# Four layers of recurrence and experts on one core: setup of layer 2's experts moved, three copies and scalings moved between engines, new prices in the instruction planner

## Chip, core and metric

One core of a Trainium2 chip runs the whole program. Its engines are TensorE (PE; its weight loads PEld), VectorE (DVE), ScalarE (ACT), GpSimd (POOL) and SyncE (SP), which here issues the transfers. The metric is the time of one execution in microseconds (us); of several runs the median is taken. The time before is 1239.51 us, the median of 3 runs (1238.63 to 1249.76).

## What is computed

Four layers on `x` of 2 x 1024 x 128, all in 32 bits. In each, the normalised input goes through a mixing part and a gating part:

```python
for layer in range(4):
    xn = layernorm(x)
    x = x + attn[layer](xn) * silu(ffn[layer](xn))
```

- Layer 0: a gated residual, a quantisation over groups, and a selective recurrence `h = h * exp(dt * A) + dt * x * B`, `y = sum(h * C)` over 16 states of 256 channels; beside it 8 experts with three matrices each.
- Layer 1: attention with global queries and keys; 8 experts, two of them chosen for each token.
- Layer 2: a convolution of 4 taps, then a recurrence in chunks with 32 heads of 64 and 128 states; 8 experts of width 64 with gelu and a shared one.
- Layer 3: causal attention and a feed-forward of width 512.

```python
# layer 2, the recurrence in chunks
Y_diag = (einsum('bcln,bcsn->bcls', C, B) * exp(segsum(A))) @ (dt * h)   # inside a chunk
states = einsum('bclhn,bclhp->bchpn', B * decay, dt * h)                 # what a chunk leaves
states = scan(states, decay_of_chunk)                                    # over the chunks
Y_off  = einsum('bcln,bchpn->bclhp', C, states) * exp(A_cum)             # from chunks before
y = (Y_diag + Y_off + D * h) * silu(gate)
```

## The kernel before

**Tiling.** Tokens lie in 16 tiles of 128. Features by tokens are handled in pieces of 512 columns, one bank of PSUM. A product that must be accurate is split: both factors into a rounded and a rest part (`split`, lines 541 and 542), and three matmuls (`mm3`, lines 553 to 555).

**Layer 0** (`take_1` to `take_5`, `inputs`, `step`). Each batch is done in two halves of 512 tokens, and each half in 16 steps `n` of two state groups. `take_1` makes `u`, the normalised input of a half, in four tiles with a scale and a shift for each row (line 946), turns it on TensorE, and hands it on. It runs two halves ahead, at step 14. `step` makes `dA` on ScalarE (line 1183), scans twice on VectorE (line 1184), and in the first half of each batch copies the last columns of `hs` into `last` (line 1186), from which the second half goes on. Then GpSimd multiplies `hs` in place by C (line 1187), and TensorE adds up the states into `y_ps` (line 1194). Layer 0's experts run beside it, and layer 1 of the first batch begins near its end.

**Layer 1** of the second batch (`layer_1`) alternates exponentials of the attention (line 663) and silu of the experts (line 721) on ScalarE.

**Layer 2** first makes features, batch constants (`batch_start`) and routing for both batches, in pools called `l2f` and `l2fw`. Then come its experts. Their weights are `fW1`, split in two; `pair`, a pattern that spreads the routing over an expert's rows, made from the scratch `pairf`; and the biases `b2s`. They stand in the pool `l2m`, opened after the features' pools; `pairf` takes the room of the gelu tiles `hw` in the pool `l2mw`. Lines 1581 to 1591 are the experts: `pb` from `pair`, `ph` from `fW1`, then the outputs.

Then 2 x 16 blocks of 128 features go through `front` (projection, convolution, silu), `weights` (the matrix `M` inside a chunk), `states` and `tail`. `states` turns `h` into `htok`, scales it on GpSimd (`hdd`, line 1662), multiplies to `u_ps` (line 1673), scans over chunks on VectorE (`st`, line 1674), and copies the states, turned about, into `stc` (line 1676): the first half on GpSimd, the second on ScalarE. `st` is read with a step of four elements. `tail` needs `M`, `htok` and `stc` for `yd_ps` and `yo_ps` (lines 1696 and 1701), adds and gates on VectorE and GpSimd (lines 1704 to 1713), and projects four blocks at a time (line 1720).

**What sets the order.** The program text gives only the dependencies. `_issue_order` plans every engine's queue: `_price` gives each instruction a duration, `_forward` runs a list planner over all engines with the tiles' rooms, `_backward` ranks instructions by the work behind them, and after 12 rounds the order with the shortest planned span is fixed, engine by engine. `SOONER` brings named parts forward. A pool whose room overlaps an older one waits, in the plan, for all of that one (`_pools_behind`); on the chip a tile waits for the tiles that it overlaps. ScalarE's queue is chosen so as to avoid changes of its function table.

## Time and profile before

| What | Value |
|---|---|
| Median of 3 runs | 1239.51 us |
| Profiled execution | 1244.13 us, span 1242.4 us |
| Layer 0: start and half 1; rest with layer 1 of batch 0 | 0 to 90; 90 to 470 |
| Layer 1 of batch 1, layer 2's first features | 411 to 625 |
| Layer 2's experts | 617 to 690 |
| Layer 2's blocks | 690 to 1157 |
| Layer 3 | 1147 to 1242 |

Times in the last five rows are from the first to the last instruction of the lines in question, so neighbours overlap. The page gives busy time by engine, then the span in 40 slices, one digit a slice:

```
PE   3797779877266888999999779899998998899998
DVE  6876997987999787678762578787897898889575
ACT  4455776765767784498743678778888778877554
POOL 6321777876657445122230257777885778887411
PEclk 9898989997667799999996889999999999998999
```

A digit is the busy share in tenths. VectorE is fuller than TensorE in slices 9 to 12, and from slice 17 on it is the other way. `PEclk` is the clock that TensorE was granted, in tenths of full speed; it falls with TensorE's activity in slices 9 to 13, and in slice 21 (652 to 683) while TensorE is busy. A row of a group reads: line, engine, operation, output and inputs with shapes, count | busy us in all, mean ns | idle us of the engine before them, and which instruction ended that idle time.

### The profile page before, as it was taken

The numbers are of one execution on the slowest core, as the hardware profiler recorded it, in microseconds if no ns is written. First come the engines' busy times: TensorE is split into PE (matmuls) and PEld (weight loads), VectorE is DVE, ScalarE is ACT, GpSimd is POOL, SyncE is SP. The second block draws the span as 40 slices with busy tenths as digits, with TensorE's granted clock in tenths as the row PEclk, the third lists the DMA queues.
The fourth block names the chain that finished last, engine by engine and source line by source line (L and its number), as shares of the span: only waits on it lengthen the run. The fifth ranks groups of instructions, "written<-read, shape, count | busy, mean of one in ns | idle before, by whom it ended". The sixth has DMA issues, their size and how long they took to land.

```text
span 1242.4 us, 18110 instructions
## 1 busy us (share of the span) xinstructions
PE 1044.9 (84%) x6415; PEld 754.5 (61%) x6415; DVE 980.4 (79%) x1618; ACT 862.0 (69%) x1258; POOL 687.5 (55%) x614
## 2 busy tenths in 40 slices
PE   3797779877266888999999779899998899998998
PEld 3564335444033666788766556667675767777687
DVE  6876997987999787678762578787897898889575
ACT  4455776765767784498743678778888778877554
POOL 6321777876657445122230257777885778887411
PEclk9898989997667799999996889999999999998999
DMA  3015343335342113110120323444443443442000
GB/s 104 7 38 143 100 150 130 115 132 171 132 153 93 51 44 97 41 40 17 58 80 7 104 72 85 113 114 131 123 115 90 108 111 93 116 115 63 18 9 26
DMA packets 58846, 109.15 MB, mean 88 GB/s; under 512 B 6274, under 2 KB 31746, under 8 KB 58628
## 3 DMA queue, kind: packets, MB, share of 16 engines
q1 hardware_dynamic: 58756, 108.00, 29.3%
q8 instruction: 51, 0.84, 0.3%
q14 instruction: 39, 0.32, 0.1%
HBM read 91.59 MB, written 14.29 MB: 85 GB/s over the span
## 4 chain that ended last, share of the span: by engine, by line
PE 37%; DVE 21%; ACT 11%; issue 5%; DMA 3%; POOL 2%; SPq 0%; DVEq 0%; POOLq 0%; ACTq 0%
DVE hs L1184 3%; DVE h L1350 3%; PE y_ps L730 3%; PE wo_ps L1720 3%; PE u_ps L1673 3%; PE yd_ps L1696 2%; DVE st L1674 2%; PE yo_ps L1701 2%; PE in_ps L553 2%; PE in_ps L555 2%; PE in_ps L554 2%; PE y_ps L1589 1%; PE e_ps L1637 1%; ACT L721 1%; PE ht_ps L1658 1%
## 5 line engine op out<-in xcount | busy, mean ns | idle before, releaser
L1187 POOL TENSOR_TENSOR hs<-hs,bc 128x1024 f32<-128x1024 f32 x64 | 153.5, 2403 | 97.0 <-DVE hs L1184 41.6
L1350 DVE SCALAR_TENSOR_TENSOR h<-in_ps,w,h 128x1023 f32<-128x1023 f32 (+2 forms) x96 | 121.9, 1272 | 26.1 <-ACT h L1347 25.7
L1183 ACT ACTIVATE dA<-dd,negA 128x512 f32<-128x512 f32 x128 | 87.5, 689 | 50.6 <-DVE hs L1184 43.9
L730 PE MATMUL y_ps<-w2e,hh 128*128 128x128 f32 x512 | 79.8, 293 | 14.5 <-DVE acc L735 6.0
L1674 DVE TENSOR_TENSOR_SCAN st<-cd,u_ps 128x512 f32<-128x512 f32 x64 | 77.7, 1213 | 17.3 <-PE u_ps L1673 9.7
L730 PEld LDWEIGHTS y_ps<-w2e,hh 128*128 128x128 f32 x512 | 72.0, 203 | 30.2 <-DVE hh L722 11.3
L1640 DVE SCALAR_TENSOR_TENSOR M<-e_ps,GT 128x1024 f32<-128x1024 f32 x64 | 76.9, 1214 | 15.7 <-ACT e_ps L1638 13.8
L1662 POOL TENSOR_TENSOR hdd<-htok,dtd 128x512 f32<-128x512 f32 x64 | 68.2, 1067 | 37.5 <-ACT htok L1661 34.5
L1184 DVE TENSOR_TENSOR_SCAN hs<-dA,last,dBx 128x512 f32<-128x512 f32 x64 | 79.5, 1268 | 7.4 <-PE y_ps L1194 4.0
L1707 POOL TENSOR_TENSOR h<-h,so 128x384 f32<-128x384 f32 (+1 forms) x64 | 73.0, 1143 | 18.8 <-DVE so L1706 18.6
L1708 POOL TENSOR_TENSOR h<-h,sg 128x512 f32<-128x512 f32 x64 | 81.7, 1282 | 0.8
L1701 PE MATMUL yo_ps<-Cf,stc 128*128 128x128 f32 x448 | 75.3, 284 | 8.1 <-DVE so L1706 2.9
L1184 DVE TENSOR_TENSOR_SCAN hs<-dA,dBx 128x512 f32<-128x512 f32 x64 | 75.4, 1207 | 5.7 <-PE y_ps L1194 4.3
L1713 POOL TENSOR_TENSOR ssq<-ssq,so 128x512 f32<-128x512 f32 x60 | 76.3, 1280 | 5.0 <-ACT so L1712 4.7
L1701 PEld LDWEIGHTS yo_ps<-Cf,stc 128*128 128x128 f32 x448 | 64.6, 193 | 19.3 <-DVE so L1706 3.9
L1696 PE MATMUL yd_ps<-M,htok 128*64 128x128 f32 x1024 | 71.8, 284 | 4.9 <-DVE wo L1722 2.5
L1673 PE MATMUL u_ps<-hdd,Btok 128*128 128x128 f32 x448 | 70.6, 281 | 6.0 <-issue 3.1
L1673 PEld LDWEIGHTS u_ps<-hdd,Btok 128*128 128x128 f32 x448 | 63.1, 193 | 18.1 <-issue 9.8
L553 PE MATMUL in_ps<-xh,w_in_l 128*128 128x512 f32 x128 | 60.8, 477 | 13.2 <-ACT sg L1620 5.1
L1175 DVE TENSOR_TENSOR dBx<-dd,B_ps 128x1024 f32<-128x1024 f32 x48 | 58.0, 1208 | 12.0 <-DMA dd<-dt 6.6
L1696 PEld LDWEIGHTS yd_ps<-M,htok 128*64 128x64 f32 x1024 | 56.1, 139 | 18.1 <-DVE wo L1722 3.6
L1638 ACT ACTIVATE e_ps<-e_ps 128x1024 f32<-128x1024 f32 x64 | 63.8, 1012 | 1.6 <-PE e_ps L1637 1.0
(533 smaller groups left out, 3220.9 us busy)
## 6 DMA issues: line engine op xcount, KB each, us to landing
bc<-BCd SPq DMA_DIRECT2D x32, 512.0 KB
cd<-Dd SPq DMA_DIRECT2D x32, 512.0 KB
so<-So SPq DMA_DIRECT2D x64, 256.0 KB
dd<-Dtd SPq DMA_DIRECT2D x28, 512.0 KB
w13f<-in_w13d_dram SPq DMA_DIRECT2D x16, 256.0 KB
Dtd<-dt SPq DMA_DIRECT2D x7, 512.0 KB
fw<-in_fwd_dram SPq DMA_DIRECT2D x16, 192.0 KB
dd<-dt SPq DMA_DIRECT2D x4, 512.0 KB
```

What stands on the lines that cost most here:

```text
L553: nc.tensor.matmul(out, wl, xh, start=start, stop=False)
L730: nc.tensor.matmul(y_ps[:, j * P : (j + 1) * P], hh[:, c, j * P : (j + 1) * P], w2e[:, c * P : (c + 1) * P], start=(c == 0), stop=(c == 1))
L1183: nc.scalar.activation(dA, dd[:, r, 0, :], AF.Exp, scale=negA[:, n, r : r + 1])
L1184: nc.vector.tensor_tensor_scan(hs[:, r, :], dA, dBx[:, r, :], last[:, n, r : r + 1] if h else 0.0, ALU.mult, ALU.add)
L1187: nc.gpsimd.tensor_tensor(hs, hs, cs.to_broadcast([P, 2, 512]), ALU.mult)
L1350: nc.vector.scalar_tensor_tensor(dst[:, n:], ps[:, : S - n], w[:, k : k + 1], dst[:, n:], ALU.mult, ALU.add)
L1640: nc.vector.scalar_tensor_tensor(M, ps, 3.0e38, G, ALU.min, ALU.mult)
L1673: nc.tensor.matmul(pv[:, j, :], Btok[:, c, :], hdd[:, c, :], start=True, stop=True)
L1674: nc.vector.tensor_tensor_scan(st.rearrange("p f j -> p (f j)"), cd[:, half].rearrange("p h w -> p (h w)"), ps, 0.0, ALU.mult, ALU.add)
L1696: nc.tensor.matmul(yd[64 * k : 64 * (k + 1), j * P : (j + 1) * P], htok[:, 4 * q + j, 64 * k : 64 * (k + 1)], Ms[q][:, k, j * P : (j + 1) ...
L1701: nc.tensor.matmul(yo[:, j * P : (j + 1) * P], stc[:, c - 1, :], Cf[:, c * P : (c + 1) * P], start=True, stop=True)
L1708: nc.gpsimd.tensor_tensor(y, y, sg[:, cols], ALU.mult)
```

## The change

Four things, and the order of all queues with them, as the planner runs anew.

1. The experts' weights of layer 2 move from after the features to before them, into a pool `l2m` that opens before `l2f`. The raw `fW1` borrows the room of `xnT`, the scratch `pairf` that of `v2`, both in `l2f`. The gelu tiles' pool `l2mw` stays where it was in the text, and shifts in memory by 2560 bytes.
2. The states' second half and `last` are copied by GpSimd, not by ScalarE.
3. `u` is scaled on ScalarE, not on VectorE and GpSimd in turn.
4. `_price` gets other durations: a fixed cost higher by 107 ns for ScalarE and by 81 ns for VectorE, prices of their own for scans, for narrow and stepped matmuls, and a lower one for GpSimd's copies.

```diff
 def _price(op, reads, writes, in_psum):
...
-        return 2 + 0.4167 * (max(n, 2 * rows) if "float32r" in str(ins.ins[0].dtype) else 4 * max(n, rows))
+        odd = 215.0 if reads[0].ap[0][1] % 32 else 250.0 if any(abs(list(a.ap)[-1][0]) > 1 for a in reads) else 0.0
+        return odd + 2 + 0.4167 * (max(n, 2 * rows) if "float32r" in str(ins.ins[0].dtype) else 4 * max(n, rows))
...
     if op.engine == "Activation":
-        return (52 if in_psum(reads[0]) else 93) + 0.8333 * n + 93 * (scalars + len(writes) - 1)
+        return (159 if in_psum(reads[0]) else 200) + 0.8333 * n + 93 * (scalars + len(writes) - 1)
     if op.engine == "DVE":
...
-        fast = ins.opcode in ("TensorScalarPtr", "TensorCopy") and full <= 1 and not any(map(in_psum, reads + writes))
-        return 69 + (0.5208 if fast else 1.0417) * n + 61 * min(scalars, 2)
+        near = any(map(in_psum, reads + writes))
+        if getattr(ins, "is_tensor_tensor_scan", False):
+            return 130 + (2.1 if near else 2.4) * n
+        fast = ins.opcode in ("TensorScalarPtr", "TensorCopy") and full <= 1 and not near
+        share = 1.0 if near else 1.2
+        return 150 + (0.5208 if fast else 1.0417) * share * n + 61 * min(scalars, 2)
     if ins.opcode == "TensorTensor":
-        return 120 + 2.16 * n
+        return 120 + 2.3 * n
...
-    return 112 + (3.3 if ins.opcode == "TensorCopy" else 1.0) * n
+    return 112 + (2.0 if ins.opcode == "TensorCopy" else 1.0) * n
...
                 for j, t in enumerate(ts):
-                    eng = nc.gpsimd if j % 2 else nc.vector
-                    eng.tensor_scalar(u[:, j, :], qx[:, t, :], rinv[:, j : j + 1], shift[:, j : j + 1], ALU.mult, ALU.add)
+                    nc.scalar.activation(u[:, j, :], qx[:, t, :], AF.Identity, bias=shift[:, j : j + 1], scale=rinv[:, j : j + 1])
...
                 if h == 0:
-                    nc.scalar.copy(last[:, n, :], hs[:, :, 511])
+                    nc.gpsimd.tensor_copy(last[:, n, :], hs[:, :, 511])
...
-        with pool_of("w2early", side="right") as pe, pool_of("l2f", side="right") as pf, pool_of("l2fw", bufs=2, side="right") as pw, lead:
+        with pool_of("w2early", side="right") as pe, pool_of("l2m", side="right") as pex, pool_of("l2f", side="right") as pf, pool_of("l2fw", bufs=2, side="right") as pw, lead:
...
+            mark("moe_2_weights")
+            fW1 = split_pair(pex, apart(pf, "fW1", "xnT"), "fW1")
+            pairf = pf.tile([P, 2, 4, 2, 64], F32, name="pairf", tag="v2", bufs=2)[:16]
...
+            pair = pex.tile([16, 4, P], F32R, name="pair")
...
             features(0)
...
-            mark("moe_2_weights")
-            pf, pw = lead.enter_context(pool_of("l2m", side="right")), lead.enter_context(pool_of("l2mw", bufs=2, side="right"))
+            pw = lead.enter_context(pool_of("l2mw", bufs=2, side="right"))
...
-            fW1 = split_pair(pf, apart(pf, "fW1", "fW1"), "fW1")
-            pairf = pw.tile([P, 2, 4, 2, 64], F32, name="pairf", tag="hw")[:16]
...
-                    (nc.scalar.copy if half else nc.gpsimd.tensor_copy)(stc[:, 4 * half : 4 + 3 * half, :], st[:, :, half:].rearrange("p f j -> p j f"))
+                    nc.gpsimd.tensor_copy(stc[:, 4 * half : 4 + 3 * half, :], st[:, :, half:].rearrange("p f j -> p j f"))
```

More of the change, by code (lines that the diff above doesn't have):

```diff
@@ L1516, in routing @@
                     nc.scalar.copy(wT[:, b * S + q * 512 : b * S + (q + 1) * 512], ps[:26, :])
+            mark("moe_2_weights")
+            fW1 = split_pair(pex, apart(pf, "fW1", "xnT"), "fW1")
+            pairf = pf.tile([P, 2, 4, 2, 64], F32, name="pairf", tag="v2", bufs=2)[:16]
+            nc.gpsimd.memset(pairf, 1.0)
+            for h in range(2):
+                nc.gpsimd.affine_select(out=pairf[:, h], in_=pairf[:, h], pattern=[[-2, 4], [-1, 2], [0, 64]], compare_op=ALU.is_equal, fill=0.0, base=-8 * h, channel_multiplier=1)
+            pair = pex.tile([16, 4, P], F32R, name="pair")
+            nc.vector.tensor_tensor(pair, pairf[:, 0].rearrange("k p a b -> k p (a b)"), pairf[:, 1].rearrange("k p a b -> k p (a b)"), ALU.add)
+            b2h = pex.tile([26, P], F32R, name="b2h")
+            b2l = pex.tile([26, P], F32, name="b2l")
+            nc.scalar.copy(b2h, W2a["b2s"][:26, :])
+            nc.vector.tensor_tensor(b2l, W2a["b2s"][:26, :], b2h.bitcast(F32), ALU.subtract)
+            low = pex.tile([26, 3], F32, name="low")
+            nc.gpsimd.affine_select(out=low[:, 0:1], in_=ones[:26, 0:1], pattern=[[0, 1]], compare_op=ALU.is_ge, fill=0.0, base=-16, channel_multiplier=1)
+            nc.gpsimd.affine_select(out=low[:, 1:2], in_=ones[:26, 0:1], pattern=[[0, 1]], compare_op=ALU.is_equal, fill=0.0, base=-24, channel_multiplier=1)
+            nc.vector.tensor_tensor(low[:, 2:3], low[:, 0:1], low[:, 1:2], ALU.subtract)
+            nc.vector.tensor_tensor(b2l, b2l, b2h.bitcast(F32), ALU.subtract)
+            b2s = pex.tile([26, P], F32R, name="b2s")
+            nc.vector.scalar_tensor_tensor(b2s, b2l, low[:, 2:3], b2h.bitcast(F32), ALU.mult, ALU.add)
             features(0)
@@ L1540, in recurrent_d4 @@
                 nc.vector.tensor_copy(Mr[32:40].rearrange("r c l -> r (c l)"), patm)
-            mark("moe_2_weights")
-            pf, pw = lead.enter_context(pool_of("l2m", side="right")), lead.enter_context(pool_of("l2mw", bufs=2, side="right"))
+            pw = lead.enter_context(pool_of("l2mw", bufs=2, side="right"))
             pm = lead.enter_context(pool_of("l2m_ps", bufs=3, space=PSUM, side="right"))
             pmy = lead.enter_context(pool_of("l2m_y", bufs=1, space=PSUM, side="right"))
-            fW1 = split_pair(pf, apart(pf, "fW1", "fW1"), "fW1")
-            pairf = pw.tile([P, 2, 4, 2, 64], F32, name="pairf", tag="hw")[:16]
-            nc.gpsimd.memset(pairf, 1.0)
-            for h in range(2):
-                nc.gpsimd.affine_select(out=pairf[:, h], in_=pairf[:, h], pattern=[[-2, 4], [-1, 2], [0, 64]], compare_op=ALU.is_equal, fill=0.0, base=-8 * h, channel_multiplier=1)
-            pair = pf.tile([16, 4, P], F32R, name="pair")
-            nc.vector.tensor_tensor(pair, pairf[:, 0].rearrange("k p a b -> k p (a b)"), pairf[:, 1].rearrange("k p a b -> k p (a b)"), ALU.add)
-            b2h = pf.tile([26, P], F32R, name="b2h")
-            b2l = pf.tile([26, P], F32, name="b2l")
-            nc.scalar.copy(b2h, W2a["b2s"][:26, :])
-            nc.vector.tensor_tensor(b2l, W2a["b2s"][:26, :], b2h.bitcast(F32), ALU.subtract)
-            low = pf.tile([26, 3], F32, name="low")
-            nc.gpsimd.affine_select(out=low[:, 0:1], in_=ones[:26, 0:1], pattern=[[0, 1]], compare_op=ALU.is_ge, fill=0.0, base=-16, channel_multiplier=1)
-            nc.gpsimd.affine_select(out=low[:, 1:2], in_=ones[:26, 0:1], pattern=[[0, 1]], compare_op=ALU.is_equal, fill=0.0, base=-24, channel_multiplier=1)
-            nc.vector.tensor_tensor(low[:, 2:3], low[:, 0:1], low[:, 1:2], ALU.subtract)
-            nc.vector.tensor_tensor(b2l, b2l, b2h.bitcast(F32), ALU.subtract)
-            b2s = pf.tile([26, P], F32R, name="b2s")
-            nc.vector.scalar_tensor_tensor(b2s, b2l, low[:, 2:3], b2h.bitcast(F32), ALU.mult, ALU.add)
             for q in range(NQ):
```

## The prediction

> **What bounds the kernel now.** I read the page first, then busy time by stage, then the groups of instructions by shape, the waits, and last the order of time around two places. The profiled execution took 1244.13 us (span 1242.4 and 1.7 around it), 0.37% over the median of 1239.51; sums below are made against 1244.13 and scaled at the end.

> The page's first part says that no engine is near its span:

> ```profile
> PE 1044.9 (84%) x6415; PEld 754.5 (61%) x6415; DVE 980.4 (79%) x1618; ACT 862.0 (69%) x1258; POOL 687.5 (55%) x614
> ```

> Busy time by stage (columns: stretch; length; busy us of PE, PEld, DVE, ACT, POOL; granted clock; DMA share; GB/s) shows two limits. Layer 0's recurrence (90 to 411) is VectorE's, 282.6 of 321 us; from 498 to 1150 it is TensorE's, 143.7 of 152 and 412.2 of 460 us.

> ```profile
> 90.00:411.00 321.00, 233.06 (x1167) 123.34 (x1165) 282.61 (x330) 225.49 (x378) 213.14 (x122) 0.84 0.41 131
> 498.00:650.00 152.00, 143.71 (x903) 117.00 (x902) 113.20 (x299) 108.22 (x175) 36.46 (x38) 1.00 0.15 47
> 690.00:1150.00 460.00, 412.19 (x2929) 316.17 (x2928) 381.13 (x432) 365.62 (x446) 335.56 (x326) 0.97 0.39 104
> ```

> The groups that the change moves (count, then busy us and mean ns, then idle before them):

> ```profile
> L946 DVE TENSOR_SCALAR u<-qx,ln_y,shift 128x128 f32<-128x128 f32 x8 | 8.2, 1050 | 0.0
> L852 ACT ACTIVATE qx<-X,shift,ln_y 128x128 f32<-128x128 f32 x12 | 4.7, 479 | 3.6 <-DVE shift L819 3.6
> L1186 ACT COPY last<-hs 128x2 f32<-128x2 f32 x32 | 5.9, 186 | 13.6 <-DVE hs L1184 13.6
> L1676 POOL COPY stc<-st 128x512 f32<-128x512 f32 x32 | 35.9, 1120 | 27.2 <-DVE st L1674 27.2
> L1676 ACT COPY stc<-st 128x384 f32<-128x384 f32 x32 | 28.8, 901 | 10.7 <-DVE st L1674 10.7
> ```

> The tile view of u gives the spread of those eight VectorE rows (minimum, median, maximum ns): the mean of 1050 comes from a few long ones.

> ```profile
> L946 DVE TENSOR_SCALAR u<-qx,ln_y,shift x8: 311/342/2471, 61.9 to 229.4; 128x128 f32<-128x128 f32 x8
> ```

> The waits (us in total, times, longest): over the span, of VectorE in 90 to 411, and of TensorE in 690 to 1150.

> ```profile
> POOL hs L1187 <- ACT last L1186: 31.1, 12, 8.2
> ```

> ```profile
> DVE hs L1184 <- PE y_ps L1194: 8.4, 7, 2.9
> ```

> ```profile
> PE in_ps L553 <- ACT sg L1620: 5.1, 3, 4.1
> PE ht_ps L1658 <- ACT htok L1661: 3.3, 4, 1.7
> PE yo_ps L1701 <- ACT stc L1676: 2.4, 4, 1.1
> PE e_ps L1637 <- ACT sg L1620: 1.8, 3, 1.1
> ```

> **Part by part.** A, scaling u on ScalarE. VectorE loses 8 instructions, GpSimd 8 (6.8 us), ScalarE gains 16 of the L852 row, 16 x 0.479 = 7.7 us. VectorE sets the recurrence, and 6 of its 8 lie there, between 90.5 and 229.4. These took 7.7 us of the group's 8.2 (the two before are 0.34 each); that is the worth if the long ones vanish, and 6 x 0.342 = 2.1 if their stalls fall on the next instruction instead. I take 5, between the two: the sum is measured, but the stall's owner is not shown. On ScalarE, 70% busy there, the 16 queue among the exponentials dA; only the next half's transposes wait for u, which leaves no loss to count, and the first take has four in a row, 1.9 us, and the two engines took 2.1 (61.8 to 63.9). **-5** (0 to -7.7).

> B, last columns on GpSimd. ScalarE loses 32 x 0.186 = 5.9 us. GpSimd gains 32 small copies; none of this shape exists there, and the nearest rows, 128x3 copies of the halo (L956) at 0.184 and 0.416, give 5.9 to 13.3 us; I take 0.2 each, 6.4 us. The 31.1 us that GpSimd waited for ScalarE end, because copy and product now follow each other in one queue. But GpSimd is 66% busy there, so only what reaches VectorE counts: at most the 8.4 us in which its scans waited for y_ps. I take a quarter. Queued behind the copy are the product hs and then y_ps; if that 0.2 came through in full for the half that is not hidden, it would cost 3. **-2** (-8.4 to +3).

> C, second half of the states on GpSimd. ScalarE loses 28.8 us. GpSimd's row is 1120 ns for 512 elements, 2.19 ns each, so 384 take 0.84 us and 32 of them 26.9 us. Its busy share in 690 to 1150 goes from 335.6 to 362.5 of 460, 73 to 79%; ScalarE's falls from 79 to 73%. The copy itself is as fast as before (0.84 against 0.90). On TensorE's path lie the four waits for ScalarE above, 12.6 us; a lighter queue saves at best all of them, and I take 3, a quarter, since each is ended by one late instruction and not by the load as such. Against it: behind the copy in GpSimd's queue stand hdd and the two products of h, and the copy waits behind them; a 1.28 us product ahead of every copy, with a quarter reaching TensorE, is 32 x 1.28 / 4 = 10. **-3** (-12.6 to +10).

> [...]

> D, experts' weights set up earlier. Now the scratch of pair sits in the room of the gelu tiles, which overlaps layer 1's buffers, so it is made at 617.5 to 620.5, after layer 1's last matmuls, and the first pb runs at 621.05. In the changed program pair comes before layer 1's end. TensorE had other work then and idled only 0.54 us: that is the gain; bounds 0 and 3 (the whole delay). The gelu tiles still overlap layer 1 by 6 KB, so the experts cannot start much sooner. The second place is the gap behind the first experts, in order of time:

> ```profile
> 649.86 0.32 PE L1591 MATMUL y_ps<-b2s,wT 26*128 26x128 f32 x1
> 653.11 1.19 PE L1386 MATMUL cum_ps<-Adt,gt 128*128 128x256 f32 x2 [2.93 <-DVE sel L594]
> ```

> Another 0.72 go by before er_ps (655.03), which waits for the routing's w26. As stretches again (the clock is the third column from the right),

> ```profile
> 655.00:670.00 15.00, 14.97 (x37) 9.20 (x38) 3.17 (x5) 5.35 (x9) 0.00 (x0) 0.50 0.00 0
> 670.00:675.00 5.00, 5.00 (x23) 3.82 (x23) 0.02 (x1) 0.92 (x2) 0.00 (x0) 0.75 0.00 0
> ```

> After 3.65 us of idling the clock is at a half for 17.5 us and more with TensorE full, so some 9 to 10 us are lost. The new order puts about 2.6 us of small matmuls (k_ps 0.43 and 0.42, ct_ps 0.64, half of er_ps) behind layer 1's last outputs, which would fill the first gap; but it also sets two VectorE steps that wait for ScalarE (nlog, dtd, with a table load of 1.28 between) ahead of the routing, which opens the second by some 2 us. I keep the loss. **-0.5** (-10 to +3). Early loading costs nothing: the raw weights borrow xnT's room, split by 488.5 and needed by xnT at 544.9, and W_BC, now behind them in SP's queue, is split at 520.

> [...]

> E, prices and the new order. The planner's prices come nearer to the rows (a ScalarE pass of 512 from SBUF 627 ns for 520; row L1712: 632), but price no time by themselves. What can be counted is the new queue: table loads fall from 166 to 160, by 7 up to the last dA and by 3 from there to layer 1's end, against 2 more in layer 2 and 2 in layer 3. Those before layer 1's end lie on the chain of waits, where Exp and Silu alternate:

> ```profile
> 538.76 1.28 ACT L721
> 540.05 0.60 ACT hh L721
> 540.67 1.28 ACT L663
> ```

> 3 x 1.28 = 3.8 us there; the seven in the recurrence hide beside VectorE, the four late ones beside TensorE. Bounds: all six net, -8, and as much again the other way for an order that has more waits. **-4** (-8 to +8).

> Sum: -5 - 2 - 3 - 0.5 - 4 = -14.5: 1229.6 for the profiled execution, times 1239.51/1244.13, **1225** for the median.

> **Rivals.** Hidden (0.18): the removed ScalarE work was off the path. For it: TensorE is at 94% from 498 to 650 and 90% after 690, ScalarE in no stretch of 100 us above 82%. Against it: the chain above. Only A's lower end remains, 2.1 us: 1237 (1233 to 1242).

> GpSimd becomes late in layer 2 (0.22, slower): yo_ps waits for both halves of the states, now in one queue with hdd, two products of h and ssq. Price: all 26.9 us added come onto the path, less the 11.5 of A, B, D and E, +15.4: 1255 (1246 to 1262). For it: in 1000 to 1100 GpSimd was already 81% busy. It decides once yo_ps waits more than 15 us for GpSimd's stc.

> The half clock goes (0.12): the gap at 650 stays under 2 us, 10 us more are won: 1215 (1207 to 1222). For it the 2.6 us of filling; against it the delayed routing.

> That a part does not do what it says holds for D: the weights were never in layer 1's room, only their scratch, so D is priced at next to nothing.

> **Numbers.** The sum as it stands has 0.48 (1216 to 1236). One per cent, 12.4 us, is about what can be told from no change. Below 1227 lie 0.34 of the first case and all of the last: faster 0.46; within, 0.14 and the hidden case: same 0.32; slower 0.22. The range 1209 to 1254 leaves out some 0.08 below and 0.12 above.

> **What would show it.** A: VectorE's busy time in the recurrence down by 5 or more and the last scan, now at 470, some 7 us sooner. B: no wait of hs for last. C: stc rows on GpSimd near 0.84 us, yo_ps waiting under 5 us for them. D: pair before layer 1's end, the clock still at a half after the first experts. E: 160 table loads. I am wrong if VectorE's sum falls and the scan does not end sooner, or if TensorE's idle time in layer 2 (48 us now) grows by more than 10.

## The result, and the profile after

The changed kernel takes 1250.16 us, the median of 20 runs (1242.02 to 1257.64); the kernel before, run beside it, 1242.32 (20 runs). The ratio is 1.0063, 95% interval 1.0044 to 1.0082: slower by some 0.6%, where 1225 and a gain were forecast. The profiled execution took 1251.49 us, its span is 1249.8, against 1242.4 before: 7.4 us more.

The page's busy time of the whole span. VectorE has 7 us more than before, in 8 instructions fewer; ScalarE has 31 us less, GpSimd 29 us more, as the moved copies would have it.

```profile
PE 1061.0 (85%) x6415; PEld 766.6 (61%) x6415; DVE 987.1 (79%) x1610; ACT 830.6 (66%) x1204; POOL 716.9 (57%) x670
```

Busy time by stage, with the columns of before (stretch; length; PE, PEld, DVE, ACT, POOL; granted clock; DMA share; GB/s). The figure that stands out is the clock of the second line, 0.90 where it was 1.00. TensorE's idle time in the third fell from 47.8 us to 41.5.

```profile
90.00:411.00 321.00, 241.34 (x1158) 124.89 (x1158) 290.51 (x330) 223.67 (x357) 217.45 (x148) 0.83 0.40 132
498.00:650.00 152.00, 140.05 (x802) 113.92 (x800) 104.10 (x281) 95.25 (x156) 31.29 (x31) 0.90 0.15 45
690.00:1150.00 460.00, 418.50 (x2983) 323.17 (x2982) 384.28 (x429) 343.73 (x418) 358.31 (x355) 0.98 0.39 105
```

The groups that were moved: u on ScalarE, last and the states' second half on GpSimd. The scaling costs what the row of before gave (0.484 us, for 0.479 assumed); the copies cost a little more than assumed (0.230 and 0.889 us, for 0.2 and 0.84).

```profile
L1682 POOL COPY stc<-st 128x512 f32<-128x512 f32 x32 | 35.9, 1121 | 8.5 <-DVE st L1680 8.5
L1682 POOL COPY stc<-st 128x384 f32<-128x384 f32 x32 | 28.4, 889 | 6.4 <-DVE st L1680 6.4
L1191 POOL COPY last<-hs 128x2 f32<-128x2 f32 x32 | 7.4, 230 | 39.4 <-DVE hs L1189 19.1 <-DMA dd<-Dtd 15.3 <-DVE ln_t L538 3.6
L951 ACT ACTIVATE u<-qx,shift,ln_y 128x128 f32<-128x128 f32 x16 | 7.3, 484 | 0.0
```

The tile view of u (minimum, median, maximum ns): the long ones are gone.

```profile
L951 ACT ACTIVATE u<-qx,shift,ln_y x16: 479/482/505, 69.4 to 243.1; 128x128 f32<-128x128 f32 x16
```

Waits in 90 to 411 (total, times, longest): GpSimd's copy now waits for the scans themselves, and the scans no longer wait for y_ps.

```profile
POOL last L1191 <- DVE hs L1189: 19.1, 10, 4.6
DVE hs L1189 <- ACT dA L1188: 5.0, 4, 2.5
```

TensorE's waits in 690 to 1150. For the states on GpSimd it waits 2.4 us, as long as it did for ScalarE.

```profile
PE in_ps L559 <- ACT sg L1626: 5.9, 2, 4.1
...
PE yo_ps L1707 <- POOL stc L1682: 2.4, 3, 1.2
...
PE ht_ps L1664 <- ACT htok L1667: 0.8, 2, 0.5
PE e_ps L1643 <- ACT sg L1626: 0.4, 1, 0.4
```

So where is the time? The table holds the end of an instruction, in us from the span's start, for both kernels and for two of the experiments below:

| End of | before | after | e1 | e3 |
|---|---|---|---|---|
| last scan of the recurrence | 471.2 | 460.9 | 463.5 | 461.9 |
| layer 1's last output matmul | 617.8 | 613.0 | 615.3 | 614.0 |
| layer 1's last X += acc | 625.6 | 624.7 | 627.0 | 625.7 |
| layer 2's last expert output | 689.6 | 707.0 | 694.7 | 690.7 |
| first convolution of the blocks | 693.7 | 711.2 | 699.0 | 695.0 |
| layer 3's first projection | 1156.9 | 1164.3 | 1153.1 | 1147.9 |
| last X | 1239.3 | 1246.6 | 1235.4 | 1230.2 |

The recurrence is 10.3 us sooner. 5.5 of that goes by layer 1's last output, 3.9 between it and the last addition. From there to the first convolution 86.5 us pass instead of 68.1: 18.4 lost. The blocks then take 453.1 instead of 463.2, 10.1 won; layer 3 is the same. The result is one loss of 18 us in the experts of layer 2, larger than either gain. Windows of the clock show it (columns as above):

```profile
626.00:650.00 24.00, 23.23 (x65) 15.65 (x64) 9.97 (x40) 4.61 (x8) 2.52 (x5) 0.51 0.26 71
650.00:684.00 34.00, 29.14 (x94) 21.81 (x94) 11.80 (x30) 12.83 (x19) 4.89 (x5) 0.50 0.04 16
```

The trace's clock records have TensorE at half clock from 626.4 to 684.5, 58.0 us, where before it was 652.1 to 672.5, 20.5 us. It is busy nearly throughout, but in a run of 512-column matmuls each starts 0.43 us after the one before, not 0.23. 37.5 us more at half clock are 18.8 us of work: the 18.4.

What stands at the start of that stretch? Of TensorE's waits in 612 to 632, two lie there. The first, for `hw` (the gelu of an expert's hidden values times `pb`), ends at 625.37, before the fall; the second ends at 628.45, behind it.

```profile
PE y_ps L1595 <- DVE hw L1589: 1.2, 1, 1.2
PE ph L559 <- ACT hsh L1584: 0.8, 1, 0.8
```

And VectorE's queue in order of time there. The last addition of layer 1 waits 1.90 us for acc and then takes 1.63, and the second product hw stands behind it. In the kernel before two products run first, at 622.12 and 623.19, then the addition at 624.41.

```profile
620.50 0.69 DVE L1589 TENSOR_TENSOR hw<-hw,pb 128x512 f32<-128x512 f32 x1
623.08 1.63 DVE L757 TENSOR_TENSOR X<-X,acc 128x1024 f32<-128x1024 f32 x1 [1.90 <-POOL acc L756]
624.64 0.67 DVE L1589 TENSOR_TENSOR hw<-hw,pb 128x512 f32<-128x512 f32 x1
```

The gap between the experts of the two batches, shown for before in the prediction, has shifted behind: 1.67 and 3.19 us of waiting, for 2.93 and 0.72.

```profile
671.51 1.19 PE L1391 MATMUL cum_ps<-Adt,gt 128*128 128x256 f32 x2 [1.67 <-DVE Adt L1389]
675.89 1.86 PE L1520 MATMUL er_ps<-ident,w 128*26 128x128 f32 x8 [3.19 <-DVE w L1516]
```

### The profile page after: what moved, and what is told of

Same layout as the page of the kernel before. It is cut to its first block, busy times and chain, and to the rows that moved or that the text cites. A ratio compares the mean times of both kernels' runs of the same rounds, so it can differ in the third digit from the quotient of the medians.

```text
span 1249.8 us, 18115 instructions
## 1 busy us (share of the span) xinstructions
PE 1061.0 (85%) x6415; PEld 766.6 (61%) x6415; DVE 987.1 (79%) x1610; ACT 830.6 (66%) x1204; POOL 716.9 (57%) x670
## 5 line engine op out<-in xcount | busy, mean ns | idle before, releaser
L1192 POOL TENSOR_TENSOR hs<-hs,bc 128x1024 f32<-128x1024 f32 x64 | 154.1, 2410 | 51.5 <-DVE hs L1189 27.3
L1355 DVE SCALAR_TENSOR_TENSOR h<-in_ps,w,h 128x1023 f32<-128x1023 f32 (+2 forms) x96 | 121.9, 1270 | 16.0 <-ACT h L1352 15.4
L1646 DVE SCALAR_TENSOR_TENSOR M<-e_ps,GT 128x1024 f32<-128x1024 f32 x64 | 76.6, 1215 | 15.2 <-ACT e_ps L1644 14.7
L736 PE MATMUL y_ps<-w2e,hh 128*128 128x128 f32 x512 | 76.9, 291 | 8.7 <-DVE hh L728 7.3
L1713 POOL TENSOR_TENSOR h<-h,so 128x384 f32<-128x384 f32 (+1 forms) x64 | 73.3, 1148 | 15.5 <-DVE so L1712 15.4
L1707 PE MATMUL yo_ps<-Cf,stc 128*128 128x128 f32 x448 | 70.5, 285 | 2.9 <-POOL stc L1682 2.4
L1682 POOL COPY stc<-st 128x512 f32<-128x512 f32 x64 | 64.3, 1005 | 14.9 <-DVE st L1680 14.8
L559 PE MATMUL in_ps<-xh,w_in_l 128*128 128x512 f32 x128 | 60.4, 473 | 10.7 <-ACT sg L1626 5.9
L1199 PE MATMUL y_ps<-hs,fold 128*32 128x512 f32 x256 | 54.7, 715 | 17.3 <-POOL hs L1192 17.1
```

What stands on the lines that cost most here:

```text
L736: nc.tensor.matmul(y_ps[:, j * P : (j + 1) * P], hh[:, c, j * P : (j + 1) * P], w2e[:, c * P : (c + 1) * P], start=(c == 0), stop=(c == 1))
L1192: nc.gpsimd.tensor_tensor(hs, hs, cs.to_broadcast([P, 2, 512]), ALU.mult)
L1355: nc.vector.scalar_tensor_tensor(dst[:, n:], ps[:, : S - n], w[:, k : k + 1], dst[:, n:], ALU.mult, ALU.add)
L1646: nc.vector.scalar_tensor_tensor(M, ps, 3.0e38, G, ALU.min, ALU.mult)
L1707: nc.tensor.matmul(yo[:, j * P : (j + 1) * P], stc[:, c - 1, :], Cf[:, c * P : (c + 1) * P], start=True, stop=True)
```

## The experiments

The theory after this: the loss is the longer half clock, begun by TensorE's wait at 624 to 625, which the planner made by putting the addition ahead of hw. The rivals: the chain itself is late, whatever the clock; or one of the four parts costs by itself. Ratios are to the kernel before, run beside each, with 95% intervals; the stretches are those of the profiled execution.

**e1, e2: one instruction moved.** After planning, one instruction is taken out of VectorE's queue and put in elsewhere; e1 from the changed kernel, e2 the mirror from the kernel before.

```diff
+    for what, where, side in moves:
+        order.remove(op)
+        order.insert(order.index(ref) + side, op)
# e1: (second hw, last X += acc, 0)   e2: (last X += acc, second hw, 0)
```

> The changed kernel with one instruction moved in VectorE's queue: layer 1's last X += acc stands behind the second product hw of layer 2's first expert quarter, as in the kernel before, not ahead of it. Theory (the loss is the longer stretch at half clock, 58.0 us against 20.5, begun by TensorE's wait of 1.16 us for that product): TensorE no longer waits for hw at 625, the clock holds past 626 to about 650, the half-clock stretch is 20 to 35 us, the last expert output ends near 690 instead of 707, and the time is 1232 to 1242, a ratio to the kernel before of 0.992 to 1.000. Rival (the chain of the later routing and the table loads at layer 1's end is late whatever the clock): the last expert output stays at 704 to 708, the time at 1247 to 1253, ratio 1.004 to 1.008.

> The mirror of it: the kernel before with layer 1's last X += acc moved ahead of the second product hw in VectorE's queue; nothing else. Theory: TensorE waits about 1 us for hw near 625, the clock is halved at once and stays half for 45 to 60 us instead of 20.5, the first convolution starts at 702 to 712 instead of 693.7, and the time is 1248 to 1260, ratio 1.005 to 1.014. Rival (this order costs its wait and no more): 1241 to 1244, ratio 0.999 to 1.002.

e1: 1237.05 us, 0.9918 (0.9885 to 0.9951). The stretch begins at 656 again and lasts 20.5 us:

```profile
626.00:650.00 24.00, 22.32 (x121) 16.51 (x121) 15.00 (x52) 9.85 (x17) 5.97 (x9) 1.00 0.35 95
650.00:684.00 34.00, 27.52 (x96) 17.73 (x94) 12.41 (x28) 11.35 (x17) 3.65 (x3) 0.70 0.02 8
```

One VectorE instruction in another place is worth 1.4% (1.0063 to 0.9918), and the change without this accident is a gain. The last output missed its mark (694.7, for "near 690").

e2: 1248.59 us, 1.0029 (1.0002 to 1.0056), between the two expectations. In its profiled execution TensorE waits 1.82 us for hw, the clock falls at 629.6 and is back after 3.4 us, and the experts end at 689.7 as before; but there the fall in the second gap lasts only 10.2 us, against 20.5 before. The mean granted clock of its 12 runs has a median of 0.9215, against 0.926 before, and the runs part into six of 1243.7 to 1246.9 us (0.922 to 0.927) and six of 1250.3 to 1255.1 (0.914 to 0.921); the profiled one is of the first six. So the order begins a fall; that it lasts longer in some executions than in others is inferred from the mean clock, as one alone was profiled.

**e3, e5: idling filled.** Spare matmuls into a tile that nobody reads, in TensorE's queue alone; the output is computed as before.

```diff
+                    for k in range(8):
+                        nc.tensor.matmul(warm, fW1[0][:, :P], xh[:, cols], start=True, stop=True)
# e3: five ahead of the waiting y_ps, three ahead of the waiting ph; e5: two, ahead of ph alone
```

> The changed kernel with eight spare matmuls into a tile that nobody reads: five in TensorE's queue ahead of the output that waits 1.16 us for hw, three ahead of the product that waits 0.77 us behind it. All other queues, the late addition in VectorE's among them, stay as they are. Theory (the clock falls because TensorE itself is idle there, whatever it is fed with): the clock holds past 626, the half-clock stretch is 20 to 35 us, the last expert output ends at 689 to 698, the time is 1233 to 1242, ratio to the kernel before 0.992 to 0.999. Rival (it is the order of the additions and the later chain, not the clock): as the changed kernel or worse, 1248 to 1254, ratio 1.004 to 1.009.

> The changed kernel with two spare matmuls only, in TensorE's second gap (0.77 us ahead of the product ph at 628); the first gap of 1.16 us, for hw, stays. It asks what makes the stretch long. Theory (the first gap starts it, the second keeps the clock down): the clock still falls near 626 but is back within 4 to 25 us, time 1238 to 1246, ratio 0.996 to 1.001. Rival (the length does not hang on the second gap): 45 to 60 us at half clock, time 1247 to 1254, ratio 1.004 to 1.009.

e3: 1237.52 us, 0.9944 (0.9921 to 0.9966). The eight (row of the group in 612 to 632) take 2.2 us, in place of the two waits:

```profile
L1618 PE MATMUL warm<-xh,fW_h 128*128 128x512 f32 x8 | 2.2, 396 | 0.0
```

```profile
626.00:650.00 24.00, 23.92 (x129) 17.68 (x127) 14.99 (x53) 9.78 (x18) 4.77 (x9) 1.00 0.32 89
650.00:684.00 34.00, 28.04 (x114) 18.56 (x114) 13.75 (x30) 11.93 (x17) 3.65 (x3) 0.80 0.02 8
```

The y_ps that waited starts at 626.38, 1.01 later than after, and layer 1's last output ends 1.0 later too; nothing was brought forward. Yet the last expert output ends 16.3 us sooner. The clock holds to 654.9 and is then at a half for 13.7 us, less than the 20 to 35 expected. The other engines' queues, the chain and every price are those of the changed kernel; beside the spare matmuls only the clock differs. This settles it against the rival chain.

e5: 1238.61 us, 0.997 (0.9938 to 1.0002), as the theory had it, though its 12 runs fall apart: nine between 1235.0 and 1239.4 with a mean clock of 0.925 to 0.931, three between 1246.4 and 1250.3 at 0.916 to 0.919. The profiled one is of the three (20.5 us at half clock from 629.6, and 13.7 more at 663.7). So two matmuls in the second wait are worth 0.9% (1.0063 to 0.997), though the first wait still begins a fall; how long it lasts in the executions that were not profiled is not shown.

**p1 to p5: the parts.** p1 is the kernel before with the new `_price`; p2 the changed kernel with the old one; p3 the changed kernel without the early weights; p4 the kernel before with u, last and the states' copies moved; p5 with the early weights only. Their diffs are those parts of the diff above.

> The kernel before with the new prices alone (u, last, the state copies and the experts' weights stay as before). The planner then also puts X += acc ahead of the second product hw. Theory: the early half clock comes from the prices alone; without what the moved copies save, the time is 1250 to 1262, ratio 1.006 to 1.016. Rival (the prices are harmless, and a moved copy or the weights cost it): 1236 to 1245, ratio 0.995 to 1.002.

> The changed kernel with the old prices: u on ScalarE, last and both state copies on GpSimd, the experts' weights set up early. The planner then keeps X += acc behind both products hw. Theory: the clock holds to about 650 and the recurrence's gain of some 10 us is kept for the most part: 1228 to 1239, ratio 0.989 to 0.998. Rival (a moved part costs by itself): 1245 to 1255, ratio 1.002 to 1.010.

> The changed kernel with the experts' weights of layer 2 left where they were before (new prices, u on ScalarE, last and states on GpSimd stay). The planner still puts X += acc ahead of the first products hw. Theory (the early half clock comes from the prices' order, not from where the weights are set up): the half clock begins near 627 to 635 again and the time is 1246 to 1258, ratio 1.002 to 1.012. Rival (the early weights brought it): 1232 to 1241, ratio 0.991 to 0.998.

> The kernel before with u on ScalarE and last and both state copies on GpSimd, and nothing else: old prices, weights where they were. In the changed kernel with old prices, layer 2's blocks took 487 us from the first convolution to layer 3's first scores, against 463 before and 453 after. Theory (GpSimd's copies at the old price of 3.3 ns an element are planned badly, whatever the weights do): the blocks take 475 to 495 us, the last scan of the recurrence ends near 460, and the time is 1252 to 1268, ratio 1.006 to 1.019. Rival (the early weights spoil the blocks): 1230 to 1240, ratio 0.989 to 0.997.

> The kernel before with the experts' weights of layer 2 set up early, and nothing else: old prices, all copies where they were; the planner keeps X += acc behind both products hw. Theory (the early weights are harmless, the late addition lengthens the half clock): the half-clock stretch of the experts is 10 to 25 us, the time 1240 to 1246, ratio 0.998 to 1.002. Rival (the early weights themselves lengthen it, as the changed kernel without them was faster than with them): stretch over 35 us, time 1248 to 1257, ratio 1.004 to 1.012.

| | u, last, stc | weights | prices | us | ratio (interval) | last scan | blocks | at half clock in the experts |
|---|---|---|---|---|---|---|---|---|
| before | | | | 1242.32 | 1 | 471.2 | 463.2 | 20.5 |
| p5 | | x | | 1243.00 | 0.9993 (0.9973 to 1.0012) | 470.7 | 465.8 | 10.2 |
| p1 | | | x | 1259.63 | 1.0110 (1.0078 to 1.0142) | 477.2 | 458.9 | 27.3 + 20.5 |
| p4 | x | | | 1275.99 | 1.0247 (1.0219 to 1.0276) | 461.6 | 491.7 | 10.2 |
| p2 | x | x | | 1263.79 | 1.0135 (1.0101 to 1.0169) | 458.0 | 487.1 | 10.2 |
| p3 | x | | x | 1241.02 | 0.9972 (0.9947 to 0.9997) | 458.4 | 453.2 | 10.2 + 20.5 |
| after | x | x | x | 1250.16 | 1.0063 (1.0044 to 1.0082) | 460.9 | 453.1 | 58.0 |

"Blocks" is the time from the first convolution to layer 3's first projection. p1 has the time that the theory named, and p4 lies 8 us above its range. p2 was expected at 1228 to 1239 and missed by 25 us: its experts end early (last output at 682.3), but its blocks are 34 us longer than after's. p3 was expected slow and is not: its ratio is the rival's, and its early fall lasts 10.2 us.

The theory's reason does not hold in p1 and p3, although both plans put the addition ahead of hw. In neither trace does TensorE wait for hw before the early fall (635.5 in p1, 621.3 in p3). It waits for the routing `wT`, which ScalarE copies; first p1, then p3:

```profile
633.14 0.49 PE L1587 MATMUL pb<-wT,pair 16*128 16x512 f32 x1 [1.83 <-ACT wT L1522]
```

```profile
619.95 0.50 PE L1586 MATMUL pb<-wT,pair 16*128 16x512 f32 x1 [1.46 <-ACT wT L1521]
```

In p1 the addition starts only at 635.10. So the place of the addition is shown as the cause for the changed kernel alone (e1, e3); in p1 and p3 the fall begins behind another wait.

What differs in p4's blocks? In 690 to 1190 GpSimd stands longer at the head of its queue with a states' copy whose scan is not done:

```profile
POOL stc L1675 <- DVE st L1673: 44.2, 34, 5.2
```

The same row after, with the new prices:

```profile
POOL stc L1682 <- DVE st L1680: 14.8, 12, 3.0
```

But before, with half of these copies, it was 27.2, and in the blocks as a whole (first convolution to layer 3's first projection) GpSimd idles hardly longer in p4 than before, 125.2 us against 121.5. On TensorE the 28.5 us by which p4's blocks exceed those of before fall into two parts. It idles 60.4 us instead of 44.9, and it is busy for 431.3 us instead of 418.3 with as many matmuls: it is at half clock for 47.8 us of the blocks instead of 23.3, and half of the difference is 12.2. What makes TensorE idle there is not shown; its yo_ps waits only 2.3 us for the states' copies. The old price has a copy of 512 elements at 112 + 3.3 x 512 = 1802 ns, where it takes 1121; the new one has 1136. That this price spoils p4's order is an inference: only all prices together were exchanged.

**b1: prices by stage.** The planner takes the old prices up to and with the experts of layer 2 and the new ones behind them.

```diff
-        op.cost = _price(op, reads, writes, in_psum)
+        op.cost = (_price_before if stage.get(ins.name, "") in OLD else _price)(op, reads, writes, in_psum)
```

> The changed kernel, in which the planner uses the old prices for everything up to and with layer 2's experts, and the new ones from layer 2's blocks on. Theory (the new prices cost at layer 1's end, where they put X += acc ahead of hw, and pay in the blocks): the experts as in the kernel without the new prices, first convolution at 684 to 694, blocks 450 to 460 us long, time 1220 to 1231, ratio 0.981 to 0.990. Rival (the blocks were short after the change only because they began late and waited for nothing): blocks 463 to 480, time 1236 to 1250, ratio 0.994 to 1.005.

1239.11 us, 0.9949 (0.993 to 0.9969). The experts are as expected (first convolution at 685.5), the blocks are not, 464.5 us, and the rival's numbers hold. Its reason does not: e3's blocks begin at 695.0, hardly later than before's, and take 452.9. The order of the blocks came out otherwise in this plan: TensorE idles 50.4 us in them, against 38.7 in e3, which covers the difference of 11.5. The row that grew most is its wait for `M`, 13.2 us, against 4.5 in e3:

```profile
PE yd_ps L1733 <- DVE M L1677: 13.2, 6, 9.3
```

Why the planner put `M` late was not followed.

**e4, b2: the second gap filled as well.** The idling between the experts of the two batches gets spare matmuls too: e4 on the kernel before (15), b2 on e1 (26).

> The kernel before with fifteen spare matmuls in TensorE's queue, twelve ahead of cum_ps (2.93 us of idling) and three ahead of er_ps (0.72 us), in the gap between the experts of the two batches; all other queues unchanged. Theory (half clock follows from a gap in TensorE's own work, and costs about half of the stretch): the 20.5 us at half clock from 652 are gone or under 7 us, the last expert output ends at 679 to 684 instead of 689.6, the time is 1233 to 1239, ratio 0.991 to 0.996. Rival (the blocks behind it give it back, as they wait for other work): 1241 to 1246, ratio 0.998 to 1.002.

> The changed kernel with X += acc behind the second hw, as in the first experiment, and 26 spare matmuls in the gap between the experts of the two batches, eleven ahead of cum_ps (2.77 us) and fifteen ahead of er_ps (3.72 us). Theory: the clock holds through all experts, the last expert output ends at 683 to 687 instead of 694.7, the time is 1226 to 1232, ratio 0.982 to 0.988. Rival (given back in the blocks, or the clock falls all the same): 1235 to 1240, ratio 0.990 to 0.995.

Neither trace shows half clock before the last expert output. e4, then b2:

```profile
650.00:690.00 40.00, 37.47 (x193) 27.59 (x192) 14.86 (x35) 15.92 (x23) 4.93 (x5) 1.00 0.09 32
```

```profile
650.00:690.00 40.00, 39.49 (x200) 28.89 (x199) 15.77 (x35) 14.61 (x21) 4.76 (x5) 1.00 0.06 20
```

From layer 1's last output to the last expert output e4 takes 64.4 us, before 71.8; b2 72.3, e1 79.4. So 7 us each in the profiled executions, less than half of the 20.5. The last outputs themselves end at 687.1 and 689.6, later than expected (679 to 684 and 683 to 687), as layer 1 ends later in both. Of the gain e4's runs show 1239.33 us, 0.9968 (0.9943 to 0.9994), just short of the expected range. b2 has 1232.01 us, 0.9919 (0.9888 to 0.995): the lowest median of all kernels here, 0.8% under before and, by 0.9919/1.0063, 1.4% under the changed kernel. But 0.982 to 0.988 was expected, and the ratio is that of e1: the runs do not separate the two, and the 7 us of the profiled executions are not confirmed.

## Why the prediction was wrong

**The step that failed** is the second place in D: "I keep the loss." It carried the half clock of 20.5 us over unchanged, at a sum of -0.5 with bounds of -10 and +3, and looked for a change only at the gap behind the first experts. It measured 18 us the other way: the new order put layer 1's last addition ahead of hw, the wait of 1.16 us for hw began a half clock of 58.0 us, and 18.4 us were lost between that addition and the first convolution. That 1250 lies inside the stated 1209 to 1254 is the width of the range, as a gain was forecast. The rival "half clock goes" had the right mechanism and the wrong sign, and no case held that the clock might fall earlier and stay longer. VectorE's new order at 620 to 625 could be read before the run; the step counted what moved past the routing, not what moved past hw.

**A and B**, -5 and -2: the last scan ends 10.3 us sooner, and 9.6 in p4 with these copies and old prices. The sign and the mechanism held (the long u rows are gone, no scan waits for y_ps), the sum was low by 3 us; how much of it is A and how much B was not tried. The marker was badly chosen: VectorE's busy time in 90 to 411 rose, from 282.6 to 290.5; 3.8 of the 7.9 us are three more scans (116 for 113) in the fixed stretch, the rest other work. That the gain would reach the end was not tested in the prediction, and 9.4 of the 10.3 were gone by layer 1's last addition.

**C**, -3, depends on the prices. With the new ones the blocks go from 458.9 (p1) to 453.2 (p3), -5.7; with the old ones from 463.2 to 491.7 (p4), +28.5. TensorE's idle time in layer 2 did not grow. The rival "GpSimd late" named 1255 with a range that holds the result, which is luck, as its reason is not there: yo_ps waits 2.4 us for the copies, not 15. In p4 the harm is real, but it is idle time and half clock on TensorE, and yo_ps waits 2.3 us for the copies there.

**D** by itself is harmless, as predicted: 0.9993 (p5); pair is made at 484, before layer 1's end. On top of the other three it goes with 0.9972 to 1.0063 (p3 to after). In the trace the early weights let the first gelu run at 614.4, between two of layer 1's steps, and ScalarE loads five tables from 611 to 621 where it loaded four from 609 to 621. That this makes the clock fall longer was not tried.

**E**, -4: the loads fell to 160 as counted, 30 instead of 33 from layer 1's start in the second batch to its end, and yet that stretch up to its last output grew from 123.8 to 126.6 us. Counting loads was no measure of an order. By itself E is +1.1% (p1: the last scan ends 6.0 us later, and the experts' half clock is 27.3 us longer), on top of the other parts -0.7% (1.0135 to 1.0063).

The sum was also wrong in form. Each term was priced alone and added, but prices, moves and weights interact through one plan: E is worth +14 or -9 us, C -6 or +29, according to what stands beside it. "Hidden" was not the case either: recurrence and blocks gained 10 us each.

**What stays open**: what decides how long the clock stays down. It lasted 3.4 us in e2 and 58.0 after, behind gaps of 1.82 and 1.16 us. Open too is what makes TensorE idle in the blocks of p4 and p2.

## What to carry to other kernels

Before costing a new order, follow the few queues around each place where TensorE is barely fed, and ask of every wait of a microsecond whether the clock holds behind it. Here the price was not the wait (1.16 us in the changed kernel) but up to half of the stretch at half clock behind it: 18.4 us for 37.5 us more at half clock (before to after), and 7 for 20.5 in the profiled executions of e4 and b2. Where TensorE must wait, a handful of spare matmuls that fill the wait (the eight of e3 took 2.2 us) shows in one run whether the clock is the cause, and may be kept. Measured prices and moved work should be tried in all combinations, as a planner can turn either into a loss without the other.

## What was not expected of the hardware

**The clock was back after 3.4 us in e2 (from 629.6), after 20.5 before and after 58.0 in the changed kernel.** Before, the last five of the stretch's six windows were wholly busy; after, eleven windows in a row were wholly busy at half clock. So there one busy window did not bring it back.

**Where the runs of the changed kernel differed, their clock differed too.** Over the 20 runs of the changed kernel the time goes against the mean granted clock with a correlation of -0.87: 1242.0 us at 0.923, 1257.6 at 0.910, about 9 us for each hundredth. In p5, whose 12 runs lie within 4 us, there is none (0.08, at 0.920 to 0.930).
